# Down products of an FP4 feed-forward stage issued in equal shares, with eight banks where there are none, and four norm tiles moved

## The chip, the cores and the metric

The kernel runs on one core of a Trainium2 chip. The metric is the device time of one execution in microseconds. The engines are TensorE (PE; its weight loads are PEld), VectorE (DVE), ScalarE (ACT), GpSimd (POOL) and SyncE (SP, which issues most DMAs).

## The reference

Two layers run over x of 2 x 1024 rows and 512 columns. Each layer has an attention part and a feed-forward part, and after each part comes `x = layernorm(x + part(x))`. The change lies in the feed-forward part of the first layer, whose weights are FP4 codes (eight in one 32-bit word) with one scale for each output and each group of 128 inputs:

```python
gate_up = einsum('bsh,oh->bso', x, w_gu)        # 512 -> 2 x 1408
gate, up = gate_up[..., :1408], gate_up[..., 1408:]
h = silu(gate) * up
y = einsum('bsi,hi->bsh', h, w_down)            # 1408 -> 512
y = y / sqrt(mean(y * y) + 1e-6)
x = layernorm(x + y)
```

Before it stands a linear attention with 16 heads, after it a gated linear attention in chunks of 64 rows, and at the end a feed-forward part for the 512 best rows of each sequence.

## The kernel before

The 2048 rows are four blocks of 512. The first stage (attention) leaves x, normalised, in `x_t[blk]`, four tiles of 128 rows for a block. `layernorm` takes the statistics `mv`, computes the reciprocal root on POOL (line 174) and normalises each tile (line 176), there on POOL. The last tile of all is i = 7 of b = 1, so that the four norm tiles of `x_t[3]` are the last that the first stage gives to POOL.

In the FP4 stage, loop `for blk in range(NB)` (line 616), the 1408 hidden features are `NI` = 11 chunks `f` of 128. For each chunk `scaled_sum` (line 450) computes gate, and again up: for each of the four groups `k` of 128 inputs one PSUM bank gets two matmuls (the high part `x1Th` and the low part `x1Tl` of x, both 128x512), and then the bank is drained with the group's scale into the running sum `acc` in SBUF: for k = 0 by ScalarE (line 461), for the others by VectorE (line 466). With `by_three` the last bank goes by ScalarE into the single tile `spare` (line 463), which POOL adds (line 464). All eight matmul groups take their banks from `mm_bank`, which has four; the other four, `acc_bank`, are for the down products. ScalarE then applies Silu to gate (line 628), and POOL multiplies up by gate into the hidden chunk (line 629). The sums for gate and up have two rooms each, by `f % 2`, so that ScalarE's first drain of a chunk waits for POOL's product of two chunks before.

The down projection `down` (line 488) of a block runs while the next block's chunks are computed. It is a product of 2 x 2 blocks done with seven products of half size, P1 to P7 (Strassen's scheme in Winograd's form), and an eighth, P8, for the odd last chunk. A product `whole` is two halves `r` of five matmuls of 128x256 in full fp32, with a sixth, `of_last`, where it has a tail. POOL builds the sums that it needs (line 512): `S` and changed blocks of h from the chunks, and `T1`, `T2`, `T4` and a changed `B12` from the weights (`sums_of_wdn`, line 448, eight steps). VectorE and ScalarE add the banks into y (lines 523 to 546). `down` is a generator, `pieces`; each step gives one half product, 14 with matmuls and a last one. The loop takes the steps by hand: one ahead of f = 0, one between gate and up in f = 2, 4, 6 and 7, and one behind up in f = 0 to 9; in block 0 there are none. `tc.issue_after` says behind which instruction of the same engine something has to stand; otherwise a list scheduler orders the instructions of an engine, so that the order in the trace is not always that of the text. After the last block 15 further steps run, with transposes and the router's logits between them.

`Normed` ends a block: squares of y on ScalarE, the power on POOL, the scaled rows on ScalarE, the sum with x on POOL (`to_x`), statistics on VectorE and the norm tiles on POOL (line 590). `old_steps` gives these steps to the chunks of the block after the next. Behind f = 9 and f = 10 the next block's x is transposed, and `split_quarter` makes its high part (ScalarE, line 204) and its low part (VectorE, line 205).

Of the kernel before, what the change touches and what calls it, by code (L numbers as in the profile page):

```python
# [10 lines left out]
F32 = mybir.dt.float32  # L11
# [5 lines left out]
ALU = mybir.AluOpType  # L17
# [4 lines left out]
P = 128  # L22
# [4 lines left out]
NI = I_FF // P  # L27
# [46 lines left out]
def body(ctx: ExitStack, tc: tile.TileContext, a: dict, out: bass.AP):  # L74
    nc = tc.nc
# [5 lines left out]
    sp = ctx.enter_context(tc.tile_pool(name="small", bufs=3))  # L81
# [4 lines left out]
    def mm_bank(name):  # L86
        return pmm.tile([P, 512], F32, tag="mm", name=name)
# [7 lines left out]
    def const(name):  # L95
        at, n = _AT[name]
        return table[:, at : at + n]
# [9 lines left out]
    x_t = [x[:, :, :C] for x in x_row]  # L107
# [164 lines left out]
    for b in range(B):  # L272
# [88 lines left out]
        mv, qT = {}, {}  # L361
        for n in range(10):
            if n < 8:
                weighed = weigh(n)
            if n + 2 < 8:
                with tc.issue_after(weighed):
                    q[n + 2] = new_q(n + 2)
            if n >= 1 and n <= 8:
                i = n - 1
                blk = 2 * b + i // 4  # L370
                if i % 4 == 0:
                    mv = sp.tile([P, 4, 2], F32, tag="mv", name="mv")
                ao = acc_bank("ao")
                project(ao, qT.pop(i), G)
                x = x_t[blk][:, i % 4]
                nc.vector.tensor_add(x, ao, x)
                row_stats(mv[:, i % 4], x)
                if i % 4 == 3:
                    layernorm(x_t[blk], mv, by=nc.gpsimd)
                unpack_some(b or i % 2)  # L380
            if n < 8:
                qT[n] = turned(n)
            if b == 1 and n in (2, 3, 4, 5):
                if n == 2:
                    parts = split_tiles(0)
                split_quarter(parts, 0, n - 2)
            if b == 0 and n == 7:
                xT[3] = load_xT(3)
# [43 lines left out]
    with tc.tile_pool(name="s2", bufs=1) as wk2:  # L432
# [14 lines left out]
                for j in (slice(0, 3), slice(3, NP)):  # L447
                    yield nc.gpsimd.tensor_sub(dst[:, j], x[:, j], y[:, j])

        def scaled_sum(f, parts, name, by_three):  # L450

            acc = rooms[name][f % 2]
            for k in range(KC):
                ps = mm_bank(f"{name}p")
                for x in parts:
                    ins = nc.tensor.matmul(  # L456
                        ps, wgu[:, k, f * P : (f + 1) * P], x[:, k], start=x is parts[0], stop=x is parts[1]
                    ).ins
                s = scale[:, k * FG + f : k * FG + f + 1]
                if k == 0:  # L460
                    nc.scalar.activation(acc, ps, AF.Copy, scale=s)  # L461
                elif k == KC - 1 and by_three:
                    nc.scalar.activation(spare, ps, AF.Copy, scale=s)  # L463
                    nc.gpsimd.tensor_add(acc, acc, spare)
                else:
                    last = nc.vector.scalar_tensor_tensor(acc, ps, s, acc, ALU.mult, ALU.add).ins  # L466
            return acc, ins, last
# [18 lines left out]
        of_S = lambda j: S[:, j]  # L486

        def down(h, y_of):

            A11, A12, A21, A22 = (h.block(e, s) for s in range(2) for e in range(2))  # L490

            def whole(name, x, w, tail=None):

                ps = acc_bank(name)
                for r in range(2):
                    cut = ps[:, 256 * r : 256 * r + 256]
                    for j in range(NP):
                        nc.tensor.matmul(  # L498
                            cut, x(j)[:, r], w[:, j], start=j == 0, stop=j == NP - 1 and tail is None
                        )  # L500
                    if tail is not None:
                        of_last(cut, r, *tail, start=False)
                    yield ps.rearrange("p (r c) -> p r c", r=2)

            def of_last(cut, r, s, o, start):
                nc.tensor.matmul(
                    cut, h.last(s)[:, r], wdn[:, NI - 1, 256 * o : 256 * o + 256], start=start, stop=True
                )

            def sums(op, dst, x, y):  # L510
                for j in range(NP):
                    ins = nc.gpsimd.tensor_tensor(dst(j), x(j), y(j), op).ins
                return ins

            sums(ALU.add, of_S, A21, A22)
            for p1 in whole("P1", A11, B11):
                yield
            for p2 in whole("P2", A12, B21, (0, 0)):
                yield
            for p5 in whole("P5", of_S, T1):  # L520
                yield
            c11, c12, c21, c22 = y_of()
            nc.scalar.copy(c21, p1)
            nc.vector.tensor_add(c11, c21, p2)
            ins = sums(ALU.subtract, of_S, of_S, A11)
            for p4 in whole("P4", A22, T4, (1, 0)):
                yield
            with tc.issue_after(ins):
                sums(ALU.subtract, A21, A11, A21)
            for p6 in whole("P6", of_S, T2):  # L530
                yield
            nc.vector.tensor_add(c12, c21, p6)
            sums(ALU.subtract, A12, A12, of_S)
            for p7 in whole("P7", A21, B12):
                yield
            nc.vector.tensor_add(c21, c12, p7)
            nc.vector.tensor_add(c12, c12, p5)
            nc.vector.tensor_add(c22, c21, p5)
            nc.vector.tensor_add(c21, c21, p4)
            p8 = acc_bank("P8")  # L540
            for r in range(2):
                of_last(p8[:, 256 * r : 256 * r + 256], r, 1, 1, start=True)
            for p3 in whole("P3", A12, B22, (0, 1)):
                yield
            nc.vector.tensor_add(c12, c12, p3)
            nc.vector.tensor_add(c22, c22, p8.rearrange("p (r c) -> p r c", r=2))

        class Normed:

# [31 lines left out]
                    row_stats(self.mv[:, i], x_t[self.blk][:, i])  # L581

            def norm(self, part):
                if 0 in part:
                    self.rs = sp.tile([P, 4], F32, tag="rs", name="rs")
                    nc.vector.tensor_scalar_add(self.rs, self.mv[:, :, 1], 1e-5)
                    nc.gpsimd.tensor_tensor(self.rs, self.rs, const("mhalf"), ALU.pow)
                for i in part:
                    x = x_t[self.blk][:, i]
                    nc.gpsimd.tensor_scalar(x, x, self.mv[:, i, 0:1], self.rs[:, i : i + 1], ALU.subtract, ALU.mult)  # L590

            def steps(self):

                return {
                    0: lambda: self.squares((0, 1)),
                    1: lambda: (self.squares((2, 3)), self.power()),
                    2: lambda: (self.scaled(), self.to_x((0, 1))),
                    3: lambda: self.to_x((2, 3)),
                    5: self.stats,
                    6: lambda: self.norm((0,)),  # L600
                    7: lambda: self.norm((1, 2)),
                    8: lambda: self.norm((3,)),
                }

            def rest(self):
# [10 lines left out]
        for blk in range(NB):  # L616
            h = Hidden(blk)
            for f in range(NI):
                if f == 0:
                    if blk:  # L620
                        with tc.issue_after(mm), tc.issue_after(hm):
                            next(pieces, None)
                gate, mm, st = scaled_sum(f, parts, "gate", False)
                if f in (2, 4, 6, 7):
                    with tc.issue_after(mm), tc.issue_after(st), tc.issue_after(hm), tc.issue_after(sl):
                        next(pieces, None)
                up, mm, st = scaled_sum(NI + f, parts, "up", blk == 0 or f >= NI - 2)
                sl = nc.scalar.activation(gate, gate, AF.Silu).ins
                hm = nc.gpsimd.tensor_mul(h.chunk(f), up, gate).ins  # L629
                with tc.issue_after(mm), tc.issue_after(st), tc.issue_after(hm), tc.issue_after(sl):  # L630
                    if f < NI - 1:
                        next(pieces, None)
                    if (blk == 0 and f < 6) or (blk == 1 and f in (3, 4)):
                        next(wsums)
                    if blk > 1 and f in old_steps:
                        old_steps[f]()
# [16 lines left out]
                old_steps = old.steps()  # L653
        Wog = place_w(1, "Wog")
        load_w(Wog, "WogT")
        for n in range(15):
            with tc.issue_after(mm), tc.issue_after(hm):
                next(pieces, None)
            if n == 0:
                old.squares(range(4))  # L660
                old.power()
            if n == 1:
                for _ in old.rest():
                    pass
            if n in (1, 2):
                turn(1, (2 * n - 2, 2 * n - 1))
            if n == 5:
                lp = logits(0)
        now.squares(range(4))
        now.power()  # L670
# [718 lines left out]
```

## Time and profile before

| what | value |
|---|---|
| median of five executions | 1032.73 us (1032.0 to 1032.8) |
| profiled execution | 1032.94 us |
| its span | 1031.1 us |
| mean granted TensorE clock | 0.995 |
| busy in the span | PE 97%, PEld 68%, DVE 64%, POOL 30%, ACT 27% |
| FP4 stage in the span | about 254.2 to 596.5 us |

Times in the profile count from the start of the span. A group's line gives the source line, the engine, the operation and its tiles, and how often it ran, and then the busy time, the mean duration in ns, and the idle time of the engine ahead of it with what ended it. Matmuls overlap, so the start of one to the start of the next is its price; an fp32 matmul of the text is two records in the trace, one of fp32r is one. A duration of a merged row is from the first start to the last end.

### The profile page before, as it was taken

The page shows a single profiled execution, that of the slowest core. Times are in us where ns is not written, and L with a number is a line of the kernel's source. Part 1 is how long each engine was busy: PE and PEld are TensorE (multiplying, and loading weights), DVE is VectorE, ACT ScalarE, POOL GpSimd, SP SyncE. Part 2 cuts the span into 40 slices and gives each one's busy share as a digit, 9 for nine tenths or more (in the row PEclk, how much of TensorE's full clock was granted, in tenths as well). Part 3 has the DMA queues.
Part 4 walks back from the last instruction along what each step waited for, and adds up shares of the span by engine and source line. Part 5 has one row for each costly group of instructions (what it writes and reads, how often), then busy time and mean ns, then how long its engine had stood idle before and what let it go on. Part 6 is the DMA issues. An engine that isn't in the chain of part 4 may idle for free.

```text
span 1031.1 us, 10943 instructions
## 1 busy us (share of the span) xinstructions
PE 1001.4 (97%) x4061; PEld 704.4 (68%) x4061; DVE 655.2 (64%) x1225; ACT 282.1 (27%) x469; POOL 304.4 (30%) x281
## 2 busy tenths in 40 slices
PE   8999999999799999999999999999999999999996
PEld 3454444545457887887888955687687688888885
DVE  1246745376676667677585249446688886689744
ACT  2223232222453224325324043242121123221000
POOL 1100351003973434474565403101005003000022
PEclk9999999999899999999999999999999999999999
DMA  9611123110000000000003050000002422140011
GB/s 344 196 45 56 42 70 98 31 31 0 1 1 0 1 1 1 1 1 1 1 1 92 1 214 1 1 1 1 1 1 82 124 81 82 41 140 24 1 41 41
DMA packets 25688, 48.81 MB, mean 47 GB/s; under 512 B 4652, under 2 KB 6316, under 8 KB 25123
## 3 DMA queue, kind: packets, MB, share of 16 engines
q1 hardware_dynamic: 22995, 42.85, 12.7%
q0 software_dynamic: 1920, 4.22, 1.1%
q10 hardware_dynamic: 720, 1.05, 0.3%
q8 instruction: 32, 0.52, 0.2%
q14 instruction: 21, 0.17, 0.1%
HBM read 39.70 MB, written 10.52 MB: 49 GB/s over the span
## 4 chain that ended last, share of the span: by engine, by line
PE 74%; DVE 9%; issue 8%; ACT 5%; POOL 3%; DMA 0%; POOLq 0%; DVEq 0%; ACTq 0%
PE P L498 11%; PE yp L1133 9%; PE hp L1054 7%; PE upp L456 6%; PE qp L210 5%; PE xk L279 5%; PE ao L210 5%; PE gatep L456 5%; PE kp L210 4%; DVE gate L466 3%; PE ao L937 3%; PE go L893 2%; PE kp L296 1%; ACT gate L461 1%; PE lp L423 1%
## 5 line engine op out<-in xcount | busy, mean ns | idle before, releaser
L466 DVE SCALAR_TENSOR_TENSOR gate<-gatep,scale,gate 128x512 f32<-128x512 f32 x132 | 98.9, 749 | 57.4 <-ACT gate L461 47.2
L174 POOL TENSOR_TENSOR rs<-rs,table 128x4 f32<-128x4 f32 (+1 forms) x22 | 20.6, 940 | 337.6 <-DVE rs L173 337.2
L466 DVE SCALAR_TENSOR_TENSOR up<-upp,scale,up 128x512 f32<-128x512 f32 x115 | 86.1, 748 | 25.6 <-ACT up L461 18.1
L456 PE MATMUL gatep<-x1Th,wgu 128*128 128x512 f32 x176 | 78.0, 443 | 6.7 <-ACT b L463 5.8
L456 PE MATMUL upp<-x1Th,wgu 128*128 128x512 f32 x176 | 78.0, 443 | 3.2 <-ACT up L461 0.9
L456 PE MATMUL gatep<-x1Tl,wgu 128*128 128x512 f32 x176 | 70.5, 400 | 0.0
L456 PE MATMUL upp<-x1Tl,wgu 128*128 128x512 f32 x176 | 69.8, 397 | 0.0
L629 POOL TENSOR_TENSOR h<-up,gate 128x512 f32<-128x512 f32 x32 | 41.2, 1287 | 85.3 <-DVE up L466 84.3
L498 PE MATMUL P<-wdn,h 128*128 128x256 f32 x256 | 61.4, 380 | 0.0
L210 PE MATMUL ao<-G,qT 128*128 128x512 f32 x128 | 57.6, 595 | 0.0
L210 PE MATMUL qp<-Wq,x0T 128*128 128x512 f32 x128 | 57.6, 592 | 0.0
L279 PE MATMUL xk<-k,x 128*128 128x512 f32 x128 | 56.7, 592 | 0.0
L937 PE MATMUL ao<-W1o,uT 128*128 128x512 f32 x128 | 55.6, 592 | 0.0
L456 PEld LDWEIGHTS upp<-x1Th,wgu 128*128 128x128 f32 x176 | 33.4, 190 | 29.2 <-DVE gate L466 14.8
L498 PEld LDWEIGHTS P<-wdn,h 128*128 128x128 f32 x256 | 47.6, 190 | 7.8 <-issue 0.7
L461 ACT ACTIVATE gate<-gatep,scale 128x512 f32<-128x512 f32 x44 | 30.3, 688 | 80.0 <-PE gatep L456 62.1
L841 POOL TENSOR_TENSOR sum<-sum,sq 128x512 f32<-128x512 f32 x12 | 18.5, 1539 | 108.0 <-issue 84.5
L456 PEld LDWEIGHTS gatep<-x1Th,wgu 128*128 128x128 f32 x176 | 33.3, 189 | 20.5 <-ACT b L463 9.3
L279 PEld LDWEIGHTS xk<-k,x 128*128 128x128 f32 x128 | 24.3, 190 | 30.6 <-issue 29.9
L264 DVE SCALAR_TENSOR_TENSOR k<-kp,e 128x512 f32<-128x512 f32 x16 | 11.0, 691 | 53.7 <-ACT e L263 49.3
L210 PEld LDWEIGHTS ao<-G,qT 128*128 128x128 f32 x128 | 24.0, 190 | 30.0 <-issue 28.7
L461 ACT ACTIVATE up<-upp,scale 128x512 f32<-128x512 f32 x44 | 30.2, 686 | 51.2 <-PE upp L456 50.7
(335 smaller groups left out, 2134.6 us busy)
## 6 DMA issues: line engine op xcount, KB each, us to landing
pk<-in_gu SPq DMA_DIRECT2D x16, 352.0 KB, 3.8
x<-in_x SPq DMA_DIRECT2D x4, 1024.0 KB, 12.8
w<-in_w SPq DMA_DIRECT2D x1, 4096.0 KB, 14.6
xs<-picked SPq DMA_DIRECT2D x4, 1024.0 KB, 5.2
out<-x SPq DMA_DIRECT2D x4, 1024.0 KB, 4.3
w<-in_w SPq DMA_DIRECT2D x4, 1024.0 KB, 6.6
x0T<-in_xT SPq DMA_DIRECT2D x3, 1024.0 KB, 8.9
pk<-in_dn SPq DMA_DIRECT2D x11, 256.0 KB, 3.5
```

The lines of the kernel that those rows point to most:

```text
L174: power = nc.gpsimd.tensor_tensor(rs[:, :n], rs[:, :n], const("mhalf")[:, :n], ALU.pow).ins
L210: nc.tensor.matmul(ps, lhs[:, k], w[:, k], start=start and k == 0, stop=stop and k == KC - 1)
L279: nc.tensor.matmul(acc[c], x_t[2 * b + i // 4][:, i % 4, c * P : (c + 1) * P], k, start=i == 0, stop=i == 7)
L456: ins = nc.tensor.matmul(ps, wgu[:, k, f * P : (f + 1) * P], x[:, k], start=x is parts[0], stop=x is parts[1]).ins
L461: nc.scalar.activation(acc, ps, AF.Copy, scale=s)
L466: last = nc.vector.scalar_tensor_tensor(acc, ps, s, acc, ALU.mult, ALU.add).ins
L498: nc.tensor.matmul(cut, x(j)[:, r], w[:, j], start=j == 0, stop=j == NP - 1 and tail is None)
L629: hm = nc.gpsimd.tensor_mul(h.chunk(f), up, gate).ins
L893: nc.tensor.matmul(ps[:, 256 * m : 256 * m + 256], w[:, k, m], b[:, k, 256 * half : 256 * half + 256], start=k == 0, stop=k == KC - 1,)
L937: nc.tensor.matmul(ao[i], uT[blk][:, k, i * P : (i + 1) * P], W1o[:, k], start=n == 0, stop=n == 3)
L1054: nc.tensor.matmul(ps[:, 256 * j : 256 * j + 256], w[:, k, 2 * g + j], x[:, k], start=k == 0, stop=k == 1)
L1133: nc.tensor.matmul(ps[:, 256 * r : 256 * r + 256], x(r, j), w(j), start=j == 0, stop=j == NJ - 1)
```

## The change

The text of `whole` yields ahead of each matmul and returns the bank at its end, so that a step of `pieces` is one matmul, and the y adds follow directly behind the last matmul of a product. `take` takes n steps. A block takes 5 steps ahead of f = 0 (the first one issues no matmul), 9 behind f = 0, 8 behind each of f = 1 to 7, and 9 behind f = 8; none stand between gate and up, and none behind f = 9. The order of the y adds changes: P4 and P5 are added behind P6, P8 is computed ahead of P3. After the last block the steps are taken in seven shares.

`scaled_sum` gets `eight_banks`: in block 0 and for f = 9 and 10 of each block the odd k take `acc_bank`. The same condition, `alone`, decides `by_three` of up, as before.

The norm of `x_t[3]` no longer ends the first stage: `late` keeps its statistics, and `norm_tiles` issues one tile behind the chunks f = 2, 4, 6 and 8 of block 0. The eight steps of `sums_of_wdn` move from f = 0 to 5 of block 0 and f = 3, 4 of block 1 to block 1 alone (2, 2, 2, 0, 1, 1). The steps of `Normed` are placed at other chunks: all squares behind f = 0, power, scaled rows and half of the sum behind f = 1, the other half behind f = 2, statistics behind f = 4, and the tiles behind f = 5, 7 and 8. No DMA is moved.

```diff
@@ -375,7 +375,9 @@
                 x = x_t[blk][:, i % 4]
                 nc.vector.tensor_add(x, ao, x)
                 row_stats(mv[:, i % 4], x)
-                if i % 4 == 3:
+                if i == 7 and b == 1:
+                    late = mv
+                elif i % 4 == 3:
                     layernorm(x_t[blk], mv, by=nc.gpsimd)
                 unpack_some(b or i % 2)
             if n < 8:
@@ -447,11 +449,11 @@
                 for j in (slice(0, 3), slice(3, NP)):
                     yield nc.gpsimd.tensor_sub(dst[:, j], x[:, j], y[:, j])
 
-        def scaled_sum(f, parts, name, by_three):
+        def scaled_sum(f, parts, name, by_three, eight_banks):
 
             acc = rooms[name][f % 2]
             for k in range(KC):
-                ps = mm_bank(f"{name}p")
+                ps = (acc_bank if eight_banks and k % 2 else mm_bank)(f"{name}p")
                 for x in parts:
                     ins = nc.tensor.matmul(
                         ps, wgu[:, k, f * P : (f + 1) * P], x[:, k], start=x is parts[0], stop=x is parts[1]
@@ -495,12 +497,14 @@
                 for r in range(2):
                     cut = ps[:, 256 * r : 256 * r + 256]
                     for j in range(NP):
+                        yield
                         nc.tensor.matmul(
                             cut, x(j)[:, r], w[:, j], start=j == 0, stop=j == NP - 1 and tail is None
                         )
                     if tail is not None:
+                        yield
                         of_last(cut, r, *tail, start=False)
-                    yield ps.rearrange("p (r c) -> p r c", r=2)
+                return ps.rearrange("p (r c) -> p r c", r=2)
 
             def of_last(cut, r, s, o, start):
                 nc.tensor.matmul(
@@ -513,37 +517,47 @@
                 return ins
 
             sums(ALU.add, of_S, A21, A22)
-            for p1 in whole("P1", A11, B11):
-                yield
-            for p2 in whole("P2", A12, B21, (0, 0)):
-                yield
-            for p5 in whole("P5", of_S, T1):
-                yield
+            p1 = yield from whole("P1", A11, B11)
+            p2 = yield from whole("P2", A12, B21, (0, 0))
+            p5 = yield from whole("P5", of_S, T1)
             c11, c12, c21, c22 = y_of()
             nc.scalar.copy(c21, p1)
             nc.vector.tensor_add(c11, c21, p2)
             ins = sums(ALU.subtract, of_S, of_S, A11)
-            for p4 in whole("P4", A22, T4, (1, 0)):
-                yield
+            p4 = yield from whole("P4", A22, T4, (1, 0))
             with tc.issue_after(ins):
                 sums(ALU.subtract, A21, A11, A21)
-            for p6 in whole("P6", of_S, T2):
-                yield
+            p6 = yield from whole("P6", of_S, T2)
             nc.vector.tensor_add(c12, c21, p6)
+            nc.vector.tensor_add(c21, c12, p4)
+            nc.vector.tensor_add(c12, c12, p5)
             sums(ALU.subtract, A12, A12, of_S)
-            for p7 in whole("P7", A21, B12):
-                yield
-            nc.vector.tensor_add(c21, c12, p7)
-            nc.vector.tensor_add(c12, c12, p5)
-            nc.vector.tensor_add(c22, c21, p5)
-            nc.vector.tensor_add(c21, c21, p4)
+            p7 = yield from whole("P7", A21, B12)
+            nc.vector.tensor_add(c21, c21, p7)
+            nc.vector.tensor_add(c22, c12, p7)
             p8 = acc_bank("P8")
             for r in range(2):
+                yield
                 of_last(p8[:, 256 * r : 256 * r + 256], r, 1, 1, start=True)
-            for p3 in whole("P3", A12, B22, (0, 1)):
-                yield
+            nc.vector.tensor_add(c22, c22, p8.rearrange("p (r c) -> p r c", r=2))
+            p3 = yield from whole("P3", A12, B22, (0, 1))
             nc.vector.tensor_add(c12, c12, p3)
-            nc.vector.tensor_add(c22, c22, p8.rearrange("p (r c) -> p r c", r=2))
+
+        def take(pieces, n):
+            for _ in range(n):
+                next(pieces, None)
+
+        roots = {}
+
+        def norm_tiles(blk, mv, part):
+
+            if blk not in roots:
+                rs = roots[blk] = sp.tile([P, 4], F32, tag="rs", name="rs")
+                nc.vector.tensor_scalar_add(rs, mv[:, :, 1], 1e-5)
+                nc.gpsimd.tensor_tensor(rs, rs, const("mhalf"), ALU.pow)
+            for i in part:
+                x = x_t[blk][:, i]
+                nc.gpsimd.tensor_scalar(x, x, mv[:, i, 0:1], roots[blk][:, i : i + 1], ALU.subtract, ALU.mult)
 
         class Normed:
 
@@ -581,25 +595,18 @@
                     row_stats(self.mv[:, i], x_t[self.blk][:, i])
 
             def norm(self, part):
-                if 0 in part:
-                    self.rs = sp.tile([P, 4], F32, tag="rs", name="rs")
-                    nc.vector.tensor_scalar_add(self.rs, self.mv[:, :, 1], 1e-5)
-                    nc.gpsimd.tensor_tensor(self.rs, self.rs, const("mhalf"), ALU.pow)
-                for i in part:
-                    x = x_t[self.blk][:, i]
-                    nc.gpsimd.tensor_scalar(x, x, self.mv[:, i, 0:1], self.rs[:, i : i + 1], ALU.subtract, ALU.mult)
+                norm_tiles(self.blk, self.mv, part)
 
             def steps(self):
 
                 return {
-                    0: lambda: self.squares((0, 1)),
-                    1: lambda: (self.squares((2, 3)), self.power()),
-                    2: lambda: (self.scaled(), self.to_x((0, 1))),
-                    3: lambda: self.to_x((2, 3)),
-                    5: self.stats,
-                    6: lambda: self.norm((0,)),
-                    7: lambda: self.norm((1, 2)),
-                    8: lambda: self.norm((3,)),
+                    0: lambda: self.squares(range(4)),
+                    1: lambda: (self.power(), self.scaled(), self.to_x((0, 1))),
+                    2: lambda: self.to_x((2, 3)),
+                    4: self.stats,
+                    5: lambda: self.norm((0,)),
+                    7: lambda: self.norm((1,)),
+                    8: lambda: self.norm((2, 3)),
                 }
 
             def rest(self):
@@ -619,18 +626,19 @@
                 if f == 0:
                     if blk:
                         with tc.issue_after(mm), tc.issue_after(hm):
-                            next(pieces, None)
-                gate, mm, st = scaled_sum(f, parts, "gate", False)
-                if f in (2, 4, 6, 7):
-                    with tc.issue_after(mm), tc.issue_after(st), tc.issue_after(hm), tc.issue_after(sl):
-                        next(pieces, None)
-                up, mm, st = scaled_sum(NI + f, parts, "up", blk == 0 or f >= NI - 2)
+                            take(pieces, 5)
+
+                alone = blk == 0 or f >= NI - 2
+                gate, mm, st = scaled_sum(f, parts, "gate", False, alone)
+                up, mm, st = scaled_sum(NI + f, parts, "up", alone, alone)
                 sl = nc.scalar.activation(gate, gate, AF.Silu).ins
                 hm = nc.gpsimd.tensor_mul(h.chunk(f), up, gate).ins
                 with tc.issue_after(mm), tc.issue_after(st), tc.issue_after(hm), tc.issue_after(sl):
-                    if f < NI - 1:
-                        next(pieces, None)
-                    if (blk == 0 and f < 6) or (blk == 1 and f in (3, 4)):
+                    if f < NI - 2:
+                        take(pieces, 9 if f in (0, NI - 3) else 8)
+                    if blk == 0 and f in (2, 4, 6, 8):
+                        norm_tiles(3, late, (f // 2 - 1,))
+                    for _ in range((2, 2, 2, 0, 1, 1)[f] if blk == 1 and f < 6 else 0):
                         next(wsums)
                     if blk > 1 and f in old_steps:
                         old_steps[f]()
@@ -653,18 +661,18 @@
                 old_steps = old.steps()
         Wog = place_w(1, "Wog")
         load_w(Wog, "WogT")
-        for n in range(15):
+        for n, steps in enumerate((11, 12, 10, 12, 10, 10, 14)):
             with tc.issue_after(mm), tc.issue_after(hm):
-                next(pieces, None)
+                take(pieces, steps)
             if n == 0:
                 old.squares(range(4))
                 old.power()
             if n == 1:
                 for _ in old.rest():
                     pass
-            if n in (1, 2):
-                turn(1, (2 * n - 2, 2 * n - 1))
-            if n == 5:
+            if n < 2:
+                turn(1, (2 * n, 2 * n + 1))
+            if n == 2:
                 lp = logits(0)
         now.squares(range(4))
         now.power()
```

## The prediction

> **What bounds the kernel now.** I read the page, then the FP4 stage's busy time cut at its block edges, then the timeline and the chain of waits inside one block. The page first: TensorE is busy nearly all the time.
>
> ```profile
> PE 1001.4 (97%) x4061; PEld 704.4 (68%) x4061; DVE 655.2 (64%) x1225; ACT 282.1 (27%) x469; POOL 304.4 (30%) x281
> ```
>
> So no engine can get faster; only waits of TensorE can go. The busy times by stretch (columns: stretch, length, busy us and instructions of PE, PEld, DVE, ACT, POOL, granted clock, DMA share, GB/s) are blocks 0 to 3 and the down products of block 3:
>
> ```profile
> 254.20:312.90 58.70, 51.23 (x190) 32.20 (x189) 41.52 (x61) 28.86 (x46) 43.96 (x31) 0.94 0.00 1
> 312.90:393.40 80.50, 79.44 (x349) 62.89 (x348) 54.27 (x77) 25.43 (x41) 33.58 (x35) 1.00 0.00 1
> 393.40:473.80 80.40, 79.35 (x349) 63.01 (x348) 57.81 (x86) 30.19 (x53) 46.00 (x44) 1.00 0.00 1
> 473.80:553.30 79.50, 78.83 (x352) 63.37 (x351) 56.66 (x83) 32.65 (x60) 45.99 (x44) 1.00 0.05 14
> 553.30:596.50 43.20, 43.20 (x243) 38.76 (x242) 14.47 (x25) 4.76 (x10) 19.02 (x25) 1.00 0.10 31
> ```
>
> Busy time hides small waits, so I need the price of work without waits. The chain of waits in block 1 gives it where products stand between gate and up:
>
> ```profile
> 358.81 1.86 PE gatep L456 x8
> 360.67 2.16 PE P L498 x10
> 362.83 1.88 PE upp L456 x8
> 364.71 2.16 PE P L498 x10
> ```
>
> Eight gate or up matmuls are 1.87 us; ten P records are 2.16, and a down product is two records: 0.432. A block needs 22 x 1.87 = 41.1, 78 products x 0.432 = 33.7 and 16 transposes 1.8, so 76.6 us. Blocks 1 to 3 lose 3.9, 3.8 and 2.9; block 0, without products and with 8 transposes in its stretch (0.9), needs 42.0 and loses 16.7; the tail loses nothing.
>
> Where block 0 loses it, by the timeline (start, length, engine, idle before in brackets):
>
> ```profile
> 259.02 8.25 POOL L176 TENSOR_SCALAR x<-x,mv,rs 128x512 f32<-128x512 f32 x4
> 267.24 1.26 POOL L464 TENSOR_TENSOR up<-up,b 128x512 f32<-128x512 f32 x1
> 268.53 0.69 ACT L463 ACTIVATE b<-upp,scale 128x512 f32<-128x512 f32 x1 [4.96 <-POOL up L464]
> 269.27 0.79 PE L456 MATMUL gatep<-x1Th,wgu 128*128 128x512 f32 x1 [4.90 <-ACT b L463]
> ```
>
> Four norm tiles of x[3] hold POOL; its add of the spare term stands behind them, ScalarE's next write of `spare` waits for that add, and TensorE for the bank. Then the clock drops, as the stretches show:
>
> ```profile
> 264.00:269.00 5.00, 0.37 (x2) 0.00 (x0) 0.42 (x1) 0.47 (x1) 4.92 (x4) 0.74 0.00 0
> 269.00:273.00 4.00, 3.73 (x9) 2.51 (x9) 1.50 (x2) 1.59 (x3) 3.92 (x4) 0.50 0.02 4
> ```
>
> Eight matmuls take 3.70 (269.27 to 272.97) where 1.87 would do. Stall and restart are 4.9 + 1.8 = 6.7. The other 10.0 are a steady pattern; the chain comes to the same piece every third chunk:
>
> ```profile
> 277.00 1.95 PE upp L456 x6
> ...
> 290.75 1.95 PE upp L456 x6
> ...
> 304.48 1.92 PE upp L456 x6
> ```
>
> That is 13.74 / 3 = 4.58 us a chunk, where TensorE needs 3.74.
>
> In blocks 1 to 3 the loss sits where up follows gate at once, as in block 2, f = 5:
>
> ```profile
> 432.58 0.58 PE L456 MATMUL gatep<-x1Th,wgu 128*128 128x512 f32 x1
> ...
> 435.88 0.19 PEld L456 LDWEIGHTS upp<-x1Th,wgu 128*128 128x128 f32 x1 [0.56 <-DVE gate L466]
> ...
> 436.92 2.32 PE L498 MATMUL P<-T,S 128*128 128x256 f32 x10
> ...
> 438.89 0.58 PE L456 MATMUL gatep<-x1Th,wgu 128*128 128x512 f32 x1
> ```
>
> 6.31 us against 3.74 + 2.16 = 5.90: 0.4 for waiting on DVE's drain of the gate banks.
>
> **The change, part by part.**
>
> *Norm tiles.* POOL's root and four tiles (1.03 + 8.25) leave the front of block 0 and come back singly, 2.08 each, behind the h products of f = 2, 4, 6, 8. They carry no DMA. In block 0 no POOL sum of wdn is left, since its eight (four of 1.83, four of 1.29, 12.5 together) move into block 1. There POOL is busy 33.6 of 80.5, so 12.5 more is covered; each pair is traced before the product that reads it (T1 in f = 0 for P5, which begins in f = 2; T4 in f = 2 for P4 in f = 3; the last in f = 5 for P7 in f = 6). If that cover failed TensorE would wait at most the pair, 3.1. In block 0 a chunk with a norm tile costs POOL 1.29 + 1.28 + 2.08 = 4.65. Queued behind the tile is the next chunk's add, for which ScalarE's `spare` waits, and its h product, for which the room of two chunks on waits. Over a chunk of 4.0 that is 0.7 too much, and the next chunk's 2.57 gives it back. I charge 1.0 for the four, between 0 and 2.8.
>
> *Eight banks.* In block 0 and in f = 9, 10, k = 1 and 3 go to the other four banks, so TensorE can be a chunk ahead. What is late next is DVE. Its five accumulations of a chunk took 3.97 in program order (294.35 to 298.32) and 3.70 interleaved (303.67 to 307.37); I take 3.97, because gate's three form a chain. By the Trainium skill, Perfetto Trace Analysis, section Matmul Optimizations, all eight banks should be in use for the most parallelism; read as lifting the limit altogether, a chunk would fall to TensorE's 3.74 and the whole sum would be about 2.5 us better. The five rows on DVE are the nearer measure, and decide.
>
> *Block 0, summed.* DVE's first drain stays at 256.13. Eleven chunks x 3.97 = 43.7, four x1Tl subtractions (two pairs of 1.29) 2.6, small rows 0.3, POOL 1.0: the last x1Tl ends at 303.7. Before it ended at 314.41 + 1.29 = 315.7. Gain 12.0; of that 0.4 goes, because four products instead of five stand before the first gate of block 1. So 11.6, with bounds 6.7 (the POOL stall alone) and 16.7 (all waste gone).
>
> The GPSIMD Engine Reference of the Trainium skill, section 4.1, would put elementwise work on VectorE, about twice as fast for two inputs, which speaks against keeping the norm tiles on POOL. Here a tile took 2.08 on POOL and 0.54 on DVE (line 176). By the rule, four tiles on DVE would add 2.2 to the engine that bounds block 0; on POOL they cost the 1.0 above.
>
> *Equal shares.* A block's pieces become 4 products ahead of f = 0, 9 behind f = 0 and 8 behind each of the next, 9 behind f = 8 (78 in all). No matmul is added. But in f = 2, 4, 6, 7 products stood between gate and up and hid the drain at no loss; now all nine chunks pay 0.4, where four did and f = 8 paid 0.2: 3.6 instead of 1.8 a block, +5.4 in three. Bounds: 0 (waits as in the products-between chunks) and 0.75 a chunk (0.19 + 0.56, both PEld waits of f = 5), +14.9.
>
> *Chunks 9 and 10.* What is left of the loss before is theirs: 2.1, 2.0, 1.1. With eight banks TensorE needs 4 x 1.87 + 1.8 + 4 products 1.7 = 11.0 until the next block's first gate; DVE starts 1.6 in (432.58 to 434.22) and needs 2 x 3.97 + 2.6, ending at 12.1. So 1.1 in blocks 1 and 2, and 0.1 in block 3, which has no subtraction: gain 2.9.
>
> *Adds, squares, statistics.* A chunk is now 3.74 + 0.4 + 3.46 = 7.6. DVE's six drains took 434.22 to 439.05, 4.8, so 2.8 is free; the most that is put there is three y adds (2.05) in f = 6 and in f = 7, or the statistics of f = 4 (438.96 to 441.56 and 0.17: 2.8). ScalarE's squares (3.2) fit behind f = 0; its scaled rows wait in f = 1 for POOL's power and delay only up drains, which now have 3.46 of products behind them. I charge 1.0 for overruns, between 0 and 4. The tail is the same 78 products with the same fillers: 0.
>
> Sum: -11.6 + 5.4 - 2.9 + 1.0 = **-8.1 us**. The profiled execution took 1032.94 (span 1031.1 and 1.8 around it), 0.2 above the median 1032.73; against the median, 1024.6. Nothing gives it back later: from 596.5 on the stage's end passes straight into TensorE work.
>
> **The rivals.**
> - *Drains late in every equal chunk (slower).* With no products between gate and up, whatever delays DVE's or ScalarE's first gate drain is a TensorE stall in full, 27 times. At 0.3 a chunk the gain is gone; at 0.38 the kernel is slower by over 0.2%. With another 0.56, the wait shown in f = 5, it is +15.1: 1039.7. For it: that wait stands in the trace. Against: DVE has 2.8 free of 7.6. Chance 0.15.
> - *Banks were not the limit of block 0.* The chunk stays 4.58, set by ScalarE, DVE and POOL handing on; only the stall goes: -6.7 + 5.4 - 2.9 + 1.0 = -3.2, 1029.5. For it: ScalarE's waits stand in that chain. Against: DVE busy is 3.5 of 4.58. Chance 0.12.
> - *It does more.* Block 0 loses a tenth of what it loses now (-15) and equal chunks lose no more than before: -15 - 2.9 = -18, 1014.8. Chance 0.10.
> - *The two sides cancel* (block 0 between 6.7 and 9, equal chunks at 0.6): within 0.2%, 1032. Chance 0.06.
>
> **How the numbers follow.** My forecast has 0.57, with its own range 1019 to 1029. A measurement here can tell 0.2%, about 2.1 us, from no change. Faster: 0.57 + 0.12 + 0.10 = 0.79; same 0.06; slower 0.15. The range leaves out the slower rival and part of the best one: 1016.5 to 1030.5.
>
> **What would show it.** Right: no POOL line 176 before block 0's first add, no 4.9 wait, clock 1.00 there; chunk period near 4.0; block 0 about 47; blocks 1 to 3 near 81.5; gate, up and 16 records of P in turn with a wait of about 0.4 in up. Wrong: a period of 4.5 in block 0, blocks 1 to 3 over 84, or POOL again named before ScalarE's line 461 or 463.

## The result, and the profile after

The changed kernel took 1033.52 us (median of 24 runs, 1030.97 to 1034.68), the kernel before 1032.65 (44 runs). The ratio of the means is 1.0004, 95% interval 0.9999 to 1.001. That is no difference that can be told. The forecast was 1024.6, and the range 1016.5 to 1030.5 does not hold the result. The profiled execution took 1033.51, with a span of 1031.7 (before: 1032.94 and 1031.1).

In the changed kernel line 456 is now 458 (gate and up matmuls), 461 is 463 (ScalarE's drain), 464 and 466 are 466 and 468 (POOL's add, DVE's drains), 498 and 506 are 501 and 510 (down products), 628 and 629 are 634 and 635 (Silu and h product), 567/568 are 581/582 (POOL's power), 572 is 586 (scaled rows), 577 is 591 (`to_x`) and 523 is 524 (ScalarE's copy to c21). In some experiments they stand a line or two beside these; then the tile's name tells which one it is.

The page's line of busy times hardly differs: TensorE has as much work and is as busy as before.

```profile
PE 1000.1 (97%) x4061; PEld 707.4 (69%) x4061; DVE 652.3 (63%) x1225; ACT 283.9 (28%) x469; POOL 305.8 (30%) x281
```

The busy times by stretch of the changed kernel, cut as before at the first down product behind a block (blocks 0 to 3, then the down products of block 3; the second column is the length, the three last the granted clock, DMA share and GB/s). One cut, 382.30, lies 1.7 behind that product, so block 1 is 82.2 and block 2 87.7; sums over the blocks are not touched by it.

```profile
252.90:298.40 45.50, 44.40 (x194) 34.26 (x193) 38.77 (x59) 29.53 (x46) 34.44 (x25) 1.00 0.00 1
298.40:382.30 83.90, 81.90 (x358) 63.98 (x356) 55.92 (x79) 26.66 (x42) 43.16 (x43) 1.00 0.00 0
382.30:468.30 86.00, 81.41 (x342) 63.26 (x342) 55.52 (x83) 30.00 (x51) 45.71 (x44) 0.96 0.00 1
468.30:554.50 86.20, 81.91 (x351) 63.77 (x350) 56.30 (x85) 33.16 (x61) 46.72 (x46) 0.98 0.04 13
554.50:597.10 42.60, 42.60 (x239) 38.47 (x238) 15.30 (x26) 4.38 (x9) 19.33 (x24) 1.00 0.11 32
```

Block 0 is 13.2 shorter (58.7 to 45.5), although four more of the next block's transposes (0.4) fall into it, and blocks 1 to 3 together are 15.7 longer (240.4 to 256.1). The tail gives 0.6, and the stretch begins 1.3 earlier; between profiled executions of kernels that change nothing ahead of block 0 the first gate matmul stands as far apart (e2 against before: 1.2). In all +0.6, the difference of the spans. So the gain is there, and it is given back whole in blocks 1 to 3, where the clock column reads 0.96 and 0.98.

Block 0 in the chain of waits (start, length, what) and on POOL in the timeline: the norm tiles are gone from its front, and up to 265.5 the chain runs on TensorE alone, at 3.73 a chunk.

```profile
257.06 1.87 PE gatep L458 x8
258.93 1.87 PE upp L458 x8
260.80 1.86 PE gatep L458 x8
262.66 1.87 PE upp L458 x8
```
```profile
258.66 1.29 POOL L466 TENSOR_TENSOR up<-up,b 128x512 f32<-128x512 f32 x1 [12.48 <-ACT gate L463]
```

From there to 291.6 the chain runs mostly through POOL: its adds, h products and the norm tiles that now stand between them. ScalarE's drains wait for POOL again, and TensorE for ScalarE, but little (0.63, 0.22 and 0.24). In the chain and then in the timeline:

```profile
273.64 1.30 POOL h L635
274.96 0.69 ACT gate L463
```
```profile
275.70 0.50 PE L458 MATMUL upp<-x1Th,wgu 128*128 128x512 f32 x1 [0.63 <-ACT gate L463]
```

An equal chunk (block 2, f = 1) in the timeline, from gate to the next gate:

```profile
391.82 0.58 PE L458 MATMUL gatep<-x1Th,wgu 128*128 128x512 f32 x1
...
395.07 0.19 PEld L458 LDWEIGHTS upp<-x1Th,wgu 128*128 128x128 f32 x1 [0.52 <-DVE gate L468]
...
399.37 0.59 PE L458 MATMUL gatep<-x1Th,wgu 128*128 128x512 f32 x1
```

It lasts 7.55, where its matmuls need 3.73 and eight products 3.45: 0.4 lost, as forecast. The next chunk, f = 2, lasts 13.27 (in block 3: 11.94). The same view there:

```profile
398.38 1.27 POOL L635 TENSOR_TENSOR h<-up,gate 128x512 f32<-128x512 f32 x1 [6.86 <-DVE up L468]
400.00 1.03 POOL L582 TENSOR_TENSOR ms<-ms,table 128x4 f32<-128x4 f32 x1
401.06 2.56 ACT L586 ACTIVATE y<-y,ms 128x512 f32<-128x512 f32 x4 [4.53 <-POOL ms L582]
403.53 0.67 ACT L463 ACTIVATE gate<-gatep,scale 128x512 f32<-128x512 f32 x1
404.23 1.61 DVE L468 SCALAR_TENSOR_TENSOR gate<-gatep,scale,gate 128x512 f32<-128x512 f32 x2 [6.00 <-ACT gate L463]
404.25 0.79 PE L458 MATMUL upp<-x1Th,wgu 128*128 128x512 f32 x1 [2.67 <-ACT gate L463]
```

Read it downwards. POOL's h product of f = 1 waits for DVE's up drains and ends at 399.65, after the gate of f = 2 has begun (399.37). The power stands behind it and ends at 401.03. ScalarE has come to its four scaled rows at 396.53 and waits 4.53 there; gate's first drain of f = 2 stands behind them. In f = 1 that drain began 0.86 after gate's first matmul; here it begins 4.16 after it. DVE's three drains wait for it, the four gate banks stay full, and TensorE stands for 2.67 before up. Then the clock goes:

```profile
384.00:404.30 20.30, 17.23 (x72) 12.90 (x72) 8.81 (x13) 9.93 (x19) 10.45 (x12) 0.99 0.00 0
404.30:408.00 3.70, 3.70 (x8) 2.48 (x9) 3.00 (x5) 0.81 (x2) 0.05 (x1) 0.50 0.00 0
408.00:416.00 8.00, 7.87 (x30) 5.99 (x29) 2.76 (x5) 1.83 (x3) 3.72 (x3) 0.83 0.00 0
```

The third column from the right is the granted clock. It is half through the second stretch and for (1 - 0.83) x 8.0 / 0.5 = 2.7 of the third: some 6.4 us, which cost 3.2. With the wait that is 5.9 of the 6.1 that this chunk loses.

At the block's first chunk a smaller wait is new, for a room of gate sums. The rooms go by f % 2, 11 is odd, and f = 10 and the next f = 0 take the same one:

```profile
303.09 0.69 ACT L463 ACTIVATE gate<-gatep,scale 128x512 f32<-128x512 f32 x1 [2.72 <-POOL h_even L635]
```

Counting each chunk from its first gate matmul to the next one's (the last chunk, which has no next, is left out), less 0.233 for each gate or up matmul, 0.432 for each product and 0.109 for each transpose, blocks 1 to 3 lost 10.7 before and lose 26.1 now:

| chunks | lost before | lost after | difference |
|---|---|---|---|
| f = 2 of blocks 2 and 3 | 0.0 | 10.9 | +10.9 |
| f = 0 | 1.4 | 4.3 | +2.9 |
| the others of f = 1 to 7 | 3.5 | 8.3 | +4.8 |
| f = 8 to 10 | 5.9 | 2.6 | -3.3 |

The clock alone is not the reason for the miss: the runs fall into two groups by their mean clock, 1031.0 to 1031.4 at 0.997 (7 runs) and 1033.3 to 1034.7 at 0.992 to 0.995 (the others), and even the first group is 6.5 above the forecast.

### The profile page after: what moved, and what is told of

Read it like the earlier page. It is cut to its first block, busy times and chain, and to the rows that moved or that the text cites. A ratio compares the mean times of both kernels' runs of the same rounds, so it can differ in the third digit from the quotient of the medians.

```text
span 1031.7 us, 10932 instructions
## 1 busy us (share of the span) xinstructions
PE 1000.1 (97%) x4061; PEld 707.4 (69%) x4061; DVE 652.3 (63%) x1225; ACT 283.9 (28%) x469; POOL 305.8 (30%) x281
## 3 DMA queue, kind: packets, MB, share of 16 engines
q10 hardware_dynamic: 720, 1.05, 0.3%
## 4 chain that ended last, share of the span: by engine, by line
PE 73%; DVE 10%; issue 8%; ACT 4%; POOL 4%; DMA 0%; POOLq 0%; DVEq 0%; ACTq 0%
PE P L501 11%; PE yp L1141 9%; PE hp L1062 7%; PE upp L458 6%; PE qp L210 5%; PE xk L279 5%; PE ao L210 5%; PE kp L210 4%; PE gatep L458 4%; DVE gate L468 3%; PE ao L945 3%; PE go L901 2%; ACT gate L463 2%; PE lp L425 1%; PE kp L296 1%
## 5 line engine op out<-in xcount | busy, mean ns | idle before, releaser
L458 PE MATMUL upp<-x1Th,wgu 128*128 128x512 f32 x176 | 75.9, 433 | 10.6 <-ACT gate L463 7.8
L458 PE MATMUL gatep<-x1Th,wgu 128*128 128x512 f32 x176 | 74.5, 430 | 1.2 <-ACT x1Th L204 1.1
L945 PEld LDWEIGHTS ao<-W1o,uT 128*128 128x128 f32 x128 | 24.0, 190 | 28.7 <-issue 28.0
L210 PE MATMUL kp<-Wk,x0T 128*128 128x512 f32 x96 | 43.3, 593 | 0.2 <-DVE k L264 0.2
## 6 DMA issues: line engine op xcount, KB each, us to landing
x<-in_x SPq DMA_DIRECT2D x4, 1024.0 KB, 12.9
```

Of the source, the lines that this page charges most:

```text
L210: nc.tensor.matmul(ps, lhs[:, k], w[:, k], start=start and k == 0, stop=stop and k == KC - 1)
L458: ins = nc.tensor.matmul(ps, wgu[:, k, f * P : (f + 1) * P], x[:, k], start=x is parts[0], stop=x is parts[1]).ins
L945: nc.tensor.matmul(ao[i], uT[blk][:, k, i * P : (i + 1) * P], W1o[:, k], start=n == 0, stop=n == 3)
```

## The experiments

Ratios are to the kernel before, run on the same chip; 0.2% is about what can be told.

**e1: the power ahead of the chunk.** The changed kernel, but POOL's power is issued at the head of f = 1 and no longer behind that chunk's h product:

```diff
-   1: lambda: (self.power(), self.scaled(), self.to_x((0, 1))),
+   1: lambda: (self.scaled(), self.to_x((0, 1))),
...
+   if blk > 1 and f == 1:
+       old.power()
```

> The changed kernel with one edit: POOL's power of blocks 2 and 3 is issued at the head of f = 1, ahead of that chunk's h product, instead of behind it. Theory A (ScalarE's four scaled rows wait for that power and stand ahead of gate's first drain of f = 2, so that TensorE stops with four full banks): the two long chunks f = 2, 13.27 and 11.94 us in the profile of after, fall to the 7.6 of the others, about -10 in all: 1023.5 us, and the two shares of the clock under 1.00 in blocks 2 and 3 are gone. Theory B (equal shares leave no cover, so any lateness of ScalarE stalls TensorE, and 2.6 us of scaled rows are late wherever they stand): the chunks stay above 9.5, and the gain is 2 to 4: 1030 to 1031.5.

1023.54 us, ratio 0.9915 (0.9898 to 0.9931): 10.0 below the changed kernel. The timeline shows the power done a chunk earlier and gate's drain of f = 2 in its place, 7.55 after that of f = 1:

```profile
393.75 1.03 POOL L582 TENSOR_TENSOR ms<-ms,table 128x4 f32<-128x4 f32 x1
...
393.90 0.69 ACT L463 ACTIVATE gate<-gatep,scale 128x512 f32<-128x512 f32 x1 [0.52 <-PE gatep L458]
...
397.65 2.55 ACT L586 ACTIVATE y<-y,ms 128x512 f32<-128x512 f32 x4
401.45 0.69 ACT L463 ACTIVATE gate<-gatep,scale 128x512 f32<-128x512 f32 x1 [1.25 <-PE gatep L458]
```

The rows wait for nothing, both f = 2 chunks take 7.54, and the granted clock is 1.00 there. Two small instructions on POOL (0.20 and 1.03), moved in two blocks, are worth 10 us: the main cause is shown.

**e2: only the new table of steps**, in the kernel before:

```diff
-   0: lambda: self.squares((0, 1)),
-   1: lambda: (self.squares((2, 3)), self.power()),
-   2: lambda: (self.scaled(), self.to_x((0, 1))),
...
+   0: lambda: self.squares(range(4)),
+   1: lambda: (self.power(), self.scaled(), self.to_x((0, 1))),
+   2: lambda: self.to_x((2, 3)),
...
```

> The kernel before, with only the new table of the steps of Normed (squares in f = 0; power, scaled rows and half of the sum in f = 1; and so on). Theory A: ScalarE's wait for the power is there too, but in f = 2 six products (2.6 us) still stand between gate and up, so that most of it is covered: +1 to +3, 1034 to 1036. If the table alone carried the whole loss: +10, 1043. If it costs nothing: 1032.7.

1038.96 us, ratio 1.006 (1.0043 to 1.0077): +6.6, more than expected. The wait is there without equal shares:

```profile
411.15 2.56 ACT L572 ACTIVATE y<-y,ms 128x512 f32<-128x512 f32 x4 [3.68 <-POOL ms L568]
413.62 0.67 ACT L461 ACTIVATE gate<-gatep,scale 128x512 f32<-128x512 f32 x1
```

In this kernel six products (2.6) stand between gate and up of f = 2, and the two chunks still lose 1.8 and 3.8, most of what the run lost. So the cover that I had thought sufficient is too short for a gate drain that begins 4.9 after its first matmul (408.72), where 0.86 is the rule.

**e3: only the norm tiles and `sums_of_wdn`**, and **e4: only the eight banks**, each in the kernel before (the hunks of the diff, unaltered; e4 in short):

```diff
-                ps = mm_bank(f"{name}p")
+                ps = (acc_bank if eight_banks and k % 2 else mm_bank)(f"{name}p")
```

> The kernel before, with only the four norm tiles of x[3] moved into block 0 and the eight sums of wdn moved into block 1. By the prediction's first term the stall and the slow clock at the head of block 0 go: -6.7, 1026.0; block 0's chunks stay at 4.5. Rival: POOL's tiles delay the adds of the spare term later, or the moved sums delay the h products of block 1, and half or more comes back: 1029 to 1032.7.

> The kernel before, with only the eight banks in block 0 and in f = 9 and 10. If four banks set the 4.58 of a chunk in block 0, its chunks fall to 3.75 to 4.0 and chunks 9 and 10 lose less, while the POOL stall of 6.7 stays: -8 to -10, 1023 to 1025. If the drains set it and not the banks: -1 to -2, 1031.

e3: 1026.43 us, 0.9944 (0.9928 to 0.9961), -5.9. The stall goes and the chunk stays at 4.5, as expected. e4: 1026.98 us, 0.9951 (0.9934 to 0.9968), -5.4, less than expected. Its ordinary chunks of block 0 take 3.73, but the stall behind POOL stays, and with the faster chunks it costs more: f = 2 and 3 lose 8.3, all of it by the stall; before, they lost 8.1, of which some 1.7 was the loss of any two chunks there.

```profile
268.27 0.80 PE L456 MATMUL upp<-x1Th,wgu 128*128 128x512 f32 x1 [4.95 <-ACT b L463]
310.17 0.69 ACT L461 ACTIVATE gate<-gatep,scale 128x512 f32<-128x512 f32 x1 [2.71 <-POOL h_even L630]
```

The second row is the wait for a room at the first chunk of block 1, 2.71 as in the changed kernel: it comes with the eight banks. The first chunks of blocks 1 to 3 lose 3.6 here (before: 1.4), and f = 8 to 10 lose 5.3 (before: 5.9). Both, and the dearer stall, kept e4 short of its expectation.

**e8: norm tiles and eight banks together**, without equal shares and with the old table:

> The kernel before, with the moved norm tiles and the eight banks, and neither the equal shares nor the new table of steps. Alone, the tiles gave -6 and the banks -5.5. If they add up, -11.5: 1021. If eight banks only run into the POOL stall sooner and the two belong together, block 0 loses less than 3 us and both give more than their sum: -13 to -15, 1018 to 1020.

1019.59 us, 0.9874 (0.9858 to 0.9891): -12.9, a little more than e3 and e4 added (-11.3), a difference near the limit of what can be told. Block 0 is as in the changed kernel (3.73 a chunk, and the same losses behind the norm tiles). So the rest of the change, equal shares and the new table, costs 1033.52 - 1019.59 = 13.9; of that the power is 10.0, which leaves 3.9 (e1 against e8). In the traces of blocks 1 to 3, f = 1 to 7 lose 3.6 in e8 and 8.6 in e1, the first chunks 3.6 and 4.4, and f = 8 to 10 5.3 and 2.6.

**e9: only equal shares**, with the old table, four banks and the norm tiles where they were:

> The kernel before, with only the equal shares: one product a step, 8 or 9 behind each of f = 0 to 8 and none between gate and up, and the new order of the y adds; the steps of Normed stay where they were. The prediction's term: +5.4 (0.4 in nine chunks a block instead of four), 1038. If the drains come late again and again without cover: +8 or more, 1040.5 up. If the scheduler puts the products between gate and up anyway: 1032.5.

1050.89 us, 1.018 (1.0164 to 1.0197): +18.4, where the prediction had +5.4. The ordinary chunks cost the 0.4 each; the rest, 13.3, is in f = 4 of blocks 2 and 3, and it is a second wait of the same kind, again with a lower clock behind it (0.72 from 434.4 to 438.0). The timeline there (line 589 is `to_x`, 522 the copy to c21):

```profile
431.41 2.49 POOL L589 TENSOR_TENSOR x<-x,y 128x512 f32<-128x512 f32 x2
433.93 0.59 ACT L522 COPY y<-P 128x512 f32<-128x512 f32 x1 [4.62 <-POOL x L589]
434.41 0.69 ACT L461 ACTIVATE up<-upp,scale 128x512 f32<-128x512 f32 x1
435.16 0.50 PE L456 MATMUL upp<-x1Th,wgu 128*128 128x512 f32 x1 [4.28 <-ACT up L461]
```

With equal shares P5 ends in f = 3 and ScalarE comes to its copy of P1 to c21. The copy writes a room of y that `to_x` of the old rows has yet to read, and that sum stands on POOL behind the h product and the S sums of f = 3. Up's first drain stands behind the copy. So the new table, with everything a chunk earlier, is needed by the equal shares: it takes this wait away and puts the wait for the power in its place.

**e5: e1, and rooms by a running count**, so that f = 10 and the next f = 0 take different rooms:

```diff
-            acc = rooms[name][f % 2]
+            acc = rooms[name][turn_of[0] % 2]
...
+                turn_of[0] = blk * NI + f
```

> The kernel with the early power, and the rooms of gate and up alternate by the running count of chunks (blk * 11 + f) instead of by f. In it, f = 10 of a block and f = 0 of the next share a room, because 11 is odd, and ScalarE's first drain of f = 0 waits for POOL's h product of f = 10 (2.7 us in the profile of after). Theory: the losses of f = 0 (2.0, 1.2 and 1.2) fall to about 0.7, the wait for the next block's x1Tl: -2 to -3, 1021. Rival: x1Tl alone sets them: 1023.5, no change.

1022.63 us, 0.9904 (0.9888 to 0.9921): -0.9 against e1, less than expected and less than can be told. By the traces the POOL wait is gone, and the first chunks lose 2.7 in all instead of 4.4, that of block 1 1.05 instead of 2.04; there ScalarE now waits for TensorE, whose gate itself is late:

```profile
303.32 0.69 ACT L465 ACTIVATE gate<-gatep,scale 128x512 f32<-128x512 f32 x1 [1.74 <-PE gatep L460]
```

What of that is the x1Tl pair and what the drains of f = 10 was not tried apart.

**e6: e5, and four of each chunk's products between gate and up:**

```diff
+                if blk and f < NI - 2:
+                    with tc.issue_after(mm), tc.issue_after(st), tc.issue_after(hm), tc.issue_after(sl):
+                        take(pieces, 4)
...
-                        take(pieces, 9 if f in (0, NI - 3) else 8)
+                        take(pieces, 5 if f in (0, NI - 3) else 4)
```

> The kernel with early power and alternating rooms, and of each chunk's 8 or 9 products four are issued between gate and up and the rest behind up. The prediction charged 0.4 a chunk for up following gate at once (27 chunks). If that is the drain of gate's banks, four products (1.7 us) cover it: -10 to -11 against the run without the split, about 1010. Rival: the loss is in the change from one kind of matmul to the other, which is now made twice a chunk: no gain, or +5.

1010.72 us, 0.9791 (0.9774 to 0.9807): -11.9 against e5, and faster than both kernels. The other expectation, that the loss lies in the change from one kind of matmul to the other, is refuted. The chain of waits in f = 0 to 8 of block 2 names TensorE alone (f = 3 is the first four pieces, 7.18):

```profile
400.92 1.86 PE gatep L460 x8
402.78 1.73 PE P L503 x8
404.51 1.86 PE upp L460 x8
406.37 1.73 PE P L503 x8
408.10 1.99 PE gatep L460 x8
```

**e7: the changed kernel with the split alone**, the power where the change put it:

> The changed kernel with one edit: of the eight (nine) down products of each chunk f = 0 to 8 of blocks 1 to 3, four stand between gate and up and the others behind up; the power stays where the change put it. Theory A (POOL's power, queued behind an h product, holds ScalarE's scaled rows and with them gate's first drain of f = 2 for about 4.5 us, whatever TensorE does in between): the other 25 chunks gain 0.4 each, 10; the two f = 2 chunks keep a loss of 1.5 to 4 each, since four products cover 1.7 of the wait: 1033.5 - 10 - 3.5 = 1020, between 1018 and 1022. Theory B (the f = 2 loss is only that no product stands between gate and up there): the two f = 2 chunks fall to 7.2 us as well, and the time comes to that of the kernel with the split and the early power, 1010.7 to 1012 (0.9 more because the rooms are not alternated).

1015.28 us, 0.983 (0.9813 to 0.9846): neither expectation. The f = 2 chunks lose nothing (7.17), which speaks against my theory in the form that I gave it, and f = 3 and 4 of blocks 2 and 3 lose 0.9 each, 3.8 in all, which the other theory did not have. The timeline explains both:

```profile
395.47 0.69 ACT L463 ACTIVATE gate<-gatep,scale 128x512 f32<-128x512 f32 x1 [2.83 <-PE gatep L458]
396.92 1.03 POOL L582 TENSOR_TENSOR ms<-ms,table 128x4 f32<-128x4 f32 x1
397.98 2.56 ACT L586 ACTIVATE y<-y,ms 128x512 f32<-128x512 f32 x4 [1.82 <-POOL ms L582]
...
403.32 0.19 PEld L458 LDWEIGHTS gatep<-x1Th,wgu 128*128 128x128 f32 x1 [0.56 <-DVE up L468]
...
408.06 0.59 ACT L524 COPY y<-P 128x512 f32<-128x512 f32 x1 [4.73 <-POOL x L591]
```

The power still stands behind the h product, but on ScalarE gate's drain of f = 2 now comes ahead of the rows, so the wait delays up's drains only, and the four products behind up cover most of that. What they do not cover is paid by the gate of f = 3, which waits for the banks of those drains (fourth row). So the price turns on the order on ScalarE: e2, with six products between gate and up but the rows ahead of gate's drain, lost 1.8 and 3.8. The late rows also make `to_x` late, c21's copy waits for it as in e9 (last row), up's drains of f = 3 stand behind the copy, and the gate of f = 4 pays.

## Why the prediction was wrong

**The step that failed** is in "Adds, squares, statistics": the scaled rows "wait in f = 1 for POOL's power and delay only up drains, which now have 3.46 of products behind them", with 1.0 charged for overruns, between 0 and 4. The rows are issued behind f = 1's up drains, so what stands next behind them on ScalarE is the gate drain of f = 2, which has no products behind it. The price is 10.9 in the trace and 10.0 by e1, beyond the step's upper bound. It could have been worked out: the h product of a chunk ends at about the start of the next gate (399.65 against 399.37), and behind it stand 0.2 + 1.03 of power and 2.56 of rows, so gate's drain comes some 4 us after gate starts, where it is due after 0.86. The kernel before showed the first half of it, in block 2, where gate of f = 2 starts at 408.97:

```profile
408.83 1.28 POOL L629 TENSOR_TENSOR h<-up,gate 128x512 f32<-128x512 f32 x1 [4.97 <-DVE up L466]
410.48 1.03 POOL L568 TENSOR_TENSOR ms<-ms,table 128x4 f32<-128x4 f32 x1
```

In the kernel before, power and rows were a chunk apart, and I read the move as a change of place, not as one that brings a producer and its waiting reader into the same step. With that one step mended, e1 comes within 1.1 of the forecast, partly by luck: block 0 gave more than forecast, and the first chunks took 2.9 that the sum did not have.

**Block 0** was right in kind and a little better than forecast: -13.2 in the stretch against -12.0. The stall (6.7 in the prediction) came to -5.9 alone in e3. The chunk was sized too large: I took DVE's program order, 3.97, and it is TensorE's 3.73. Two chunks that stand behind a norm tile, f = 5 and 7, lose 1.2 and 0.5, where 1.0 was charged for all four tiles, between 0 and 2.8. The prediction counted eight transposes in block 0's stretch before; there were twelve, so it lost 16.3 there and not 16.7, which moves only an upper bound. The Trainium skill's Perfetto Trace Analysis, section Matmul Optimizations, asks that all eight banks be in use; this was the reading that I set aside, and e4 and e8 agree with it: the chunk falls from 4.5 to 3.73.

**Equal shares** were right for the ordinary chunk (0.4); by e1 against e8, f = 1 to 7 cost 5.0 and the whole of shares and table 3.9. But e9 shows that the 5.4 of the prediction was no price of equal shares by themselves: it held only because the table moved too. **Chunks 9 and 10** gave 3.3 with f = 8, against 2.9, but not by the eight banks that the prediction credited: these alone give 0.6 (e4, e8), equal shares alone 0.4 (e9), and only both together the 3.3. Why was not tried apart. **The first chunk of a block** was not in the sum as a cost of its own: 2.9, of which the eight banks alone bring 2.2 (e4).

So blocks 1 to 3 came to +15.7, where the prediction had 0.4 + 5.4 - 2.9 + 1.0 = +3.9. **The rivals:** late drains in every equal chunk did not come about; the drains were as late as forecast in all but two chunks, and very late there. In those two it was as that rival said, that a late first gate drain stops TensorE. The cancelling came, but not by its mechanism, which had block 0 at 6.7 to 9 and equal chunks at 0.6. "Banks were not the limit" is refuted by e4. "It does more" was near for block 0 (-15), but its equal chunks were to cost nothing, and that took the split of e6. Of the signs of being wrong, two showed: "blocks 1 to 3 over 84" (87.7 and 86.2 in blocks 2 and 3), and POOL named before ScalarE's gate drain in block 0, though little was lost by that there.

## What to carry to other kernels

When a step is moved, list for each engine what stands directly behind the instruction that will wait there, in the next chunk too: an instruction that waits costs what is held up behind it, not what it is. Put a small producer (here 1.03 on POOL) a step ahead of its reader, not in the same step behind a late product. Work that hides a drain belongs between the matmuls that fill the banks and those that need them back: shares that are equal from chunk to chunk cost 3.9 with the new table (e1 against e8), and paid only when each chunk was also cut in two (e6).

## What the runs showed of the hardware

TensorE stood for 2.67 in f = 2 and ran at a granted clock of 0.50 for some 6 us after it; in the kernel before it was 0.50 after the 4.9 in block 0. By the mean clock it did not come in every execution: that of the changed kernel was 0.997 in 7 runs and 0.992 to 0.995 in the others, with 2 to 3.7 us between them. The Trainium skill, TensorE: Matmul & The Clock Gate, Part 1, has half clock after an idle window of about 3.4 us and a window that runs freely, so that it varies from run to run. The variation agrees; the length does not, since 2.67 was enough here.

How much of e1's 10 us is wait and how much clock is known only for the profiled execution: 2 x 2.67 of wait and 3.2 of clock in block 2; by the same working 1.7 in block 3 (clock 0.68 from 491.0 to 495.5 and 0.95 from 495.5 to 500.0). In the seven runs at 0.997 the changed kernel was still 7.6 above e1 (1031.14 in the median), more than the 5.3 of the two waits; those runs have no trace, and the other 2.3 stay open.
